# Unread matmuls ahead of the first and the eighth product of a two-layer graph-attention kernel

## The chip, the cores and the metric

The kernel runs on one NeuronCore of a Trainium2 chip. Five engines work side by side, each on its own queue of instructions in program order: TensorE (PE, matrix products; its weight loads are listed as PEld), VectorE (DVE), ScalarE (ACT), GpSimd (POOL), and SyncE (SP), which here issues the DMA transfers. Engines wait for each other through semaphores. The metric is the device time of one execution in microseconds (us); smaller is better. The kernel before takes 2812.2 us, the median of three runs (2810.62 to 2812.2).

## What is computed

128 graphs of 64 nodes with 768 features go through two layers. Layer 0 is a graph attention with 12 heads of 64 and a gate; layer 1 is a masked self-attention with 6 heads of 128. Each adds its input and normalizes.

```python
# layer 0
h = jnp.einsum('bnd,ade->bane', feat_in, W)
th = jnp.tanh(h)
attn = leaky(th @ w_src + swap(th @ w_dst)); softmax over masked neighbours
feat_out = elu(attn @ h + b)
gate = jax.nn.sigmoid(feat_in @ H_w.T + H_b)
x = _layernorm(x + gate * feat_out + (1.0 - gate) * feat_in)
# layer 1
q, k, v = x @ Wq + bq, x @ Wk + bk, x @ Wv + bv   # 6 heads
ctx = softmax(q @ k.T / sqrt(128) + bias) @ v
x = _layernorm(x + ctx @ Wf + bf)
```

(The formulas are shortened; all data are float32.)

## The kernel before

The rows are handled in pairs of tiles of 128 rows, 32 pairs in all; the code calls a pair p. In layer 0 the feature product and the gate product of a pair are one matrix product of 256 rows by 768 features by 1536 columns. It isn't computed block by block: a bilinear scheme writes it as **fifteen products**, `a0` to `a14` (the list `PRODUCTS`, lines 50 to 67), of sums of input blocks with sums of weight blocks. Each product is two matmuls of 128 x 512 columns (`Fifteen.product`, line 936) that accumulate into a bank of PSUM; what a product gives is then copied or accumulated into the tile `hg` by ACT (lines 962, 964) or DVE (line 960).

Three kinds of operands have to be there before a product may start:

- the input `xT` of the pair and the weight blocks `wa` come by DMA (lines 853 to 855). For the first pair, nothing can start before they land;
- the sums of input blocks, tiles `sx`, are made by DVE and POOL (`x_sums`, line 869);
- the sums of weight blocks are made once, by DVE, 17 of them (`MADE`, line 75, issued by `made(i)`, line 865, at line L867 of the profile), each over 128 x 1024 elements. One more, a negation, is made by ACT (line 863).

The products of the first pair run in the order of `EARLY[0]`, line 135: `a0 a5 a3 a8 a6 a1 a7 a10 a9 a2 a12 a4 a11 a14 a13`. The first is `a0`, the eighth is `a10`. The order of everything is written out by hand. The main loop (line 1364) goes through `items`, a list of products of all pairs; item i is issued to TensorE by `step`, which first issues the product and then the way out of the product before it. After item i, the acts that the dictionary `plan` holds for position i are issued to the other engines. For the first pair, the weight sums are planned there (line 1345): two at the outset, one to three after each of the items 0 to 5, and the last three (14, 15, 16) after items 7, 8 and 9. The eighth product, `a10`, reads the weight sum number 13 of the list (`MADE[13]`), which is planned after item 5. Position 7 of the loop is the eighth product of the first pair.

TensorE's part of a product therefore stands in its queue as early as the program has it; the semaphores it waits for are those of the operands above.

Three names matter for the change. `ident` (line 260) is the 128 x 128 identity, made by POOL at the start and used for transposes. `hb_bc` (line 856) is the gate's bias, 768 columns, repeated over the 128 partitions by a DMA. `bank("m", ...)` (line 248) hands out one of two PSUM banks that the transposes of the probabilities use later on.

Of the kernel before, what the change touches and what calls it, by code (L numbers as in the profile page):

```python
# [211 lines left out]
def kernel(  # L212
# [33 lines left out]
    V, S, G, T = nc.vector, nc.scalar, nc.gpsimd, nc.tensor  # L246

    def bank(tag, name, bufs=2):
        return ps.tile([P, 512], F32, tag=tag, name=name, bufs=bufs)
# [10 lines left out]
    ident = const.tile([P, P], F32, name="ident")  # L260
# [114 lines left out]
    def flush():  # L375
        for job, i in behind:
            job.way_out(i)
        behind.clear()

    def step(job, i):  # L380
        job.product(i)
        flush()
        behind.append((job, i))
# [432 lines left out]
    def drain(*sides):  # L816
        for s in sides:
            for _ in s:
                pass
# [4 lines left out]
    with ExitStack() as ph, ExitStack() as ph_r:  # L824
# [3 lines left out]
        def load_rows(pool, src, n, name):  # L828
            t = pool.tile([P, n], F32, name=name, bufs=1)
            nc.sync.dma_start(out=t, in_=src.partition_broadcast(P))  # L830
            return t
# [24 lines left out]
        hb_bc = load_rows(sbr, hb, D, "hb_bc")  # L856
# [5 lines left out]
        def negated():  # L862
            S.mul(wa[:, 0], wa[:, 14], -1.0)
# [5 lines left out]
        def x_sums(eng, p, ns):  # L869
            of = A.setdefault(p, {})  # L870
            x = xTs[p]

            def operand(o):
                if isinstance(o, tuple):
                    k, t = o
                    return x[:, 2 * k : 2 * k + 2, t * P : (t + 1) * P]
                return of[o]

            for n in ns:
                a, op, b = PRODUCTS[n][1]  # L880
                of[n] = sbr.tile([P, 2, P], F32, tag=f"sx{BUFFER[n]}", name=f"sx{n}_{p}", bufs=1)
                eng.tensor_tensor(of[n], operand(a), operand(b), op)  # L882
            for n in range(NW):
                if len(PRODUCTS[n][1]) == 2:
                    of[n] = operand(PRODUCTS[n][1])

        x_sums(V, 0, (6, 9, 2, 3, 0, 5))
        negated()
        x_sums(G, 0, (8,))
# [466 lines left out]
        def job_of(p, item):  # L1356
            if item[0] == "q":
                return jobs["q"]
            if (item[0], p) not in jobs:
                jobs[item[0], p] = Fifteen(p)  # L1360
            return jobs[item[0], p]

        rest = 0
        for i, (p, item) in enumerate(items):
            if i == new_at[NP - 1]:
                drain(summing)
            step(job_of(p, item), int(item[1:]))
            for _, acts in sorted(plan.get(i, ()), key=lambda entry: entry[0]):
                for act in acts:
                    act()  # L1370
            if new_at[3] <= i < new_at[NP - 1]:
                rest -= 1
                if rest <= 0:
                    rest = next(summing, 1)
            if item[0] == "q":
                jobs["rows"].ready(int(item[1:]) + 4)
# [153 lines left out]
```

## Time and profile before

| | |
|---|---|
| median of three runs | 2812.2 us |
| the profiled execution, its own time | 2813.49 us |
| its span in the profile | 2811.7 us |
| TensorE busy | 2776.4 us, 99% of the span |
| DVE, POOL, ACT busy | 66%, 52%, 48% |
| mean granted clock of TensorE | 0.997 |

A profile is one execution, recorded instruction by instruction; its times count from the start of the span. A line of a timeline gives the start, the duration of the group, the engine, the line of code, the operation, what it writes and reads with shapes, how many there are, and in brackets how long the engine had been idle before and what released it. Matmuls overlap in the array, so the durations of a group are longer than the distance from one start to the next; the distance is what TensorE can do at most. The granted clock is the share of TensorE's full clock that the chip gave it in a stretch.

At the start the transfers and the first sums of blocks come first; TensorE's first matmul starts at 7.86 us. After seven products it pauses, and goes on at 29.62 us with the eighth. The transfer of `hb_bc` is issued at 7.88 us. POOL finishes `ident` at 1.30 us.

### The profile page before, as it was taken

To read this page: it belongs to the slowest core of one execution; us is meant where nothing else is said; L and a number is where in the kernel's file an instruction comes from. 1 tells how busy PE (TensorE), PEld (TensorE's weight loads), DVE (VectorE), ACT (ScalarE), POOL (GpSimd) and SP (SyncE) were. 2 spreads that over 40 slices of the span, in tenths; PEclk is the share of its full clock that TensorE was granted. 3 is DMA by queue.
4 is the path that set the end of the run, shared out by engine and by line. 5 is a ranking of instruction groups with operands and counts; after the bars stand their busy time and mean duration, and the time that the engine had idled before them with its cause. 6 is when DMAs were issued, how large, how long until landed. Compare 5 with 4: busy or idle time off the path is not lost.

```text
span 2811.7 us, 47352 instructions
## 1 busy us (share of the span) xinstructions
PE 2776.4 (99%) x17472; PEld 1931.9 (69%) x17472; DVE 1851.2 (66%) x3215; ACT 1357.1 (48%) x3434; POOL 1453.7 (52%) x1501
## 2 busy tenths in 40 slices
PE   7999999999999999999999999999999999999998
PEld 3455555555555555555568888888888888888887
DVE  7867877777777777867764555555555555554557
ACT  4666676766767666676753222333222333221333
POOL 5556556565655656555454345445345435345435
PEclk9999999999999999999999999999999999999999
DMA  5354444544545445333444112222212222212212
GB/s 186 110 167 155 137 159 133 173 151 143 167 138 165 147 148 166 110 125 104 170 163 161 63 52 88 91 83 80 69 48 86 91 84 80 72 50 81 91 61 83
DMA packets 198038, 325.52 MB, mean 116 GB/s; under 512 B 46896, under 2 KB 125744, under 8 KB 197808
## 3 DMA queue, kind: packets, MB, share of 16 engines
q1 hardware_dynamic: 197520, 322.10, 34.8%
q8 instruction: 139, 2.28, 0.3%
q14 instruction: 91, 0.75, 0.1%
q10 hardware_dynamic: 288, 0.39, 0.0%
HBM read 198.48 MB, written 111.15 MB: 110 GB/s over the span
## 4 chain that ended last, share of the span: by engine, by line
PE 95%; DVE 1%; ACT 0%; issue 0%; DMA 0%; POOL 0%; ACTq 0%; DVEq 0%
PE y_a L944 18%; PE z_a L944 9%; PE z_q L524 9%; PE z_k L524 9%; PE y_v L345 9%; PE z_o L571 9%; PE y_k L524 6%; PE y_q L524 6%; PE y_o L571 6%; PE z_v L345 4%; PE x_v L345 2%; PE av L1099 2%; PE cp L689 2%; PE sp L629 2%; PE pTp L1078 2%; PE x1Tp L1078 1%
## 5 line engine op out<-in xcount | busy, mean ns | idle before, releaser
L944 PE MATMUL y_a<-wa,sx 128*128 128x512 f32 x1024 | 487.3, 605 | 19.2 <-DVE sx L882 7.9
L944 PEld LDWEIGHTS y_a<-wa,sx 128*128 128x128 f32 x1024 | 189.3, 192 | 221.6 <-issue 173.4
L488 POOL TENSOR_TENSOR so<-ctxT 128x256 f32<-128x256 f32 x224 | 157.7, 728 | 287.8 <-ACT ctxT L716 286.9
L716 ACT ACTIVATE ctxT<-cp,bv_c 128x256 f32<-128x256 f32 x192 | 73.8, 486 | 451.1 <-PE cp L689 451.1
L1129 POOL TENSOR_TENSOR x<-hg,x 128x768 f32<-128x768 f32 x64 | 111.8, 1748 | 211.1 <-ACT hg L1203 211.1
L524 PE MATMUL z_q<-xs,wa 128*128 128x256 f32 x896 | 211.9, 380 | 0.0
L655 ACT ACTIVATE sc<-sc 128x512 f32<-128x512 f32 x45 | 28.4, 630 | 379.7 <-DVE sc L652 379.7
L571 PE MATMUL z_o<-wf,so 128*128 128x256 f32 x896 | 209.3, 382 | 2.4 <-DVE y L584 2.4
L1037 ACT ACTIVATE att<-dd,sd 128x64 f32<-128x64 f32 x768 | 190.4, 336 | 33.4 <-DMA dd<-dstd 33.4
L986 POOL TENSOR_TENSOR th<-th,wsd 128x768 f32<-128x768 f32 x64 | 117.1, 1829 | 167.5 <-DVE th L985 167.5
L1066 ACT ACTIVATE prob<-att,mx 128x64 f32<-128x64 f32 x768 | 190.3, 335 | 25.8 <-DVE mx L1057 24.5
L524 PE MATMUL z_k<-xs,wa 128*128 128x256 f32 x840 | 198.5, 380 | 0.0
L397 POOL TENSOR_TENSOR rs_b<-ve_b,minus_half 128x1 f32<-128x1 f32 x64 | 40.9, 638 | 302.5 <-DVE ve_b L395 289.5
L584 DVE TENSOR_TENSOR y<-y,z_o 128x256 f32<-128x256 f32 x320 | 128.6, 419 | 100.3 <-PE z_o L571 100.2
L1051 DVE COPY_PREDICATED_SCALAR att<-nadj,neg 128x768 f32 x64 | 69.2, 1081 | 182.7 <-ACT att L1037 182.6
L571 PEld LDWEIGHTS z_o<-wf,so 128*128 128x128 f32 x896 | 169.1, 190 | 26.5 <-POOL so L488 2.6
L524 PEld LDWEIGHTS z_q<-xs,wa 128*128 128x128 f32 x896 | 170.2, 190 | 22.7
L944 PE MATMUL z_a<-wa,xT 128*128 128x512 f32 x384 | 183.1, 600 | 0.0
L524 PEld LDWEIGHTS z_k<-xs,wa 128*128 128x128 f32 x840 | 160.0, 190 | 21.3
L960 DVE TENSOR_TENSOR hg<-hg,y_a 128x512 f32<-128x512 f32 x225 | 151.9, 676 | 24.2 <-PE y_a L944 18.7
L760 POOL TENSOR_TENSOR y<-y,bf_bc 128x768 f32<-128x768 f32 x64 | 114.6, 1813 | 96.8 <-issue 56.0
L488 POOL TENSOR_TENSOR xs<-r,r 128x512 f32<-128x512 f32 x112 | 146.7, 1328 | 23.7 <-PE y_k L524 12.4
(154 smaller groups left out, 6427.1 us busy)
## 6 DMA issues: line engine op xcount, KB each, us to landing
xT<-in_xT_dram SPq DMA_DIRECT2D x32, 768.0 KB, 6.9
x<-in_x_dram SPq DMA_DIRECT2D x64, 384.0 KB, 3.4
dd<-dstd SPq DMA_DIRECT2D x128, 192.0 KB, 3.4
x1d<-x SPq DMA_DIRECT2D x64, 384.0 KB, 4.9
x1Td<-x1T SPq DMA_DIRECT2D x32, 768.0 KB, 4.8
vd<-v SPq DMA_DIRECT2D x64, 384.0 KB, 3.0
r<-x1Td SPq DMA_DIRECT2D x96, 256.0 KB, 3.2
v<-vd SPq DMA_DIRECT2D x192, 128.0 KB, 3.0
```

The source lines that it names most:

```text
L345: T.matmul(to[:, : self.n], lhsT, rhs, start=kc == 0 and not more, stop=kc == HK - 1, skip_group_check=more,)
L488: G.tensor_tensor(t, self.of(x[0]), self.of(x[2]), x[1])
L524: T.matmul(b[:, half * W2 : (half + 1) * W2], w[:, kc, half * P : (half + 1) * P], x[:, kc, :], start=half == kc == 0 and not more, stop=k ...
L571: T.matmul(b[:, :W2], x[:, kc, :], w[:, kc, :], start=kc == 0 and not more, stop=kc == 1, skip_group_check=more,)
L584: V.tensor_tensor(at, at, self.banks[path][:, :W2], ALU.add if sign > 0 else ALU.subtract)
L760: G.tensor_tensor(y, y, pools["bf"], ALU.add)
L944: T.matmul(b, x[:, kc, :], wa[:, n, kc, :], start=kc == 0 and not more, stop=kc == 1, skip_group_check=more,)
L960: V.tensor_tensor(at, at, b, ALU.add if sign > 0 else ALU.subtract)
L986: G.tensor_tensor(th[:, 1, :], th[:, 1, :], wsd[:, 1, :], ALU.mult)
L1037: S.activation(att3[:, a], dd3[:, a], AF.Prelu, bias=sd[:, H0 + a : H0 + a + 1], alpha=LEAKY)
L1066: S.activation(prob[:, at * N : (at + 1) * N], att[:, a * N : (a + 1) * N], AF.Exp, bias=mx[:, a : a + 1],)
L1129: G.tensor_tensor(xp, gate_of(t), xp, ALU.mult)
```

## The change

A helper `running` issues n matmuls of `ident` with an operand into a bank of the kind "m". Nothing reads what they write. It is called twice: before the sums of the first pair with n = 22 and `ident` itself as the operand (128 columns), and in the main loop ahead of item 7 with n = 20 and 512 columns of `hb_bc`.

```diff
+        def running(name, n, rhs):
+            b = bank("m", name)
+            for _ in range(n):
+                T.matmul(b[:, : rhs.shape[-1]], ident, rhs, start=True, stop=True)
+
+        running("warm", 22, ident)
         x_sums(V, 0, (6, 9, 2, 3, 0, 5))
         negated()
         x_sums(G, 0, (8,))
...
         for i, (p, item) in enumerate(items):
             if i == new_at[NP - 1]:
                 drain(summing)
+            if i == 7:
+                running("warm7", 20, hb_bc[:, :512])
             step(job_of(p, item), int(item[1:]))
```

The order of the instructions on DVE, ACT, POOL and SP is the same as before. On TensorE, the 22 stand ahead of everything and wait for POOL's `ident`; the 20 stand between `a7` and `a10` and wait for the transfer of `hb_bc`. What `a10` waits for is unchanged.

## The prediction

> **What bounds the kernel now.** I read the page's busy rows first, then the longest waits of TensorE, then its timeline over the first 45 us, then the granted clock in stretches of the same time.
>
> ```profile
> span 2811.7 us, 47352 instructions
> PE 2776.4 (99%) x17472; PEld 1931.9 (69%) x17472; DVE 1851.2 (66%) x3215; ACT 1357.1 (48%) x3434; POOL 1453.7 (52%) x1501
> ```
>
> TensorE (PE) is busy for 2776.4 of 2811.7 us, and the chain that ended last is 95% PE. So a microsecond put into PE's stream, or taken from it, reaches the end unless a later wait of PE swallows it. PE is idle for 35.3 us in all; the list of its waits says where:
>
> ```profile
> PE y_a L944 <- DVE sx L882: 7.9, 1, 7.9
> PE y_a L944 <- DVE wa L867: 7.8, 1, 7.8
> ```
>
> The columns are total, times, longest. These are the two places that the change fills, 15.7 us together. The timeline of PE (start, duration, then the group) shows what follows each of them:
>
> ```profile
> 7.86 3.67 PE L944 MATMUL y_a<-wa,sx 128*128 128x512 f32 x4 [7.86 <-DVE sx L882]
> 11.36 1.88 PE L944 MATMUL z_a<-wa,sx 128*128 128x512 f32 x4
> 13.08 5.31 PE L944 MATMUL y_a<-wa,sx 128*128 128x512 f32 x12
> 18.23 3.60 PE L944 MATMUL z_a<-wa,xT 128*128 128x512 f32 x8
> 29.62 6.44 PE L944 MATMUL y_a<-wa,sx 128*128 128x512 f32 x8 [7.79 <-DVE wa L867]
> 35.90 1.88 PE L944 MATMUL z_a<-wa,sx 128*128 128x512 f32 x4
> ```
>
> The reader is to see two things. First, a product of the fifteen leaves **four** records (a5 is the x4 at 11.36), though its code issues two matmuls: each 512-column float32 matmul is two records. Second, the pace: from 11.36 to 13.08 four records take 1.72 us, 0.429 us each; but from 7.86 to 11.36 four take 3.50 us (0.875 each), and from 29.62 to 35.90 eight take 6.28 us (0.785 each). After each wait PE runs slow for a while. The clock rows of the second place (stretch, length, busy PE, ..., granted clock, DMA share, GB/s) say why:
>
> ```profile
> 25.00:29.60 4.60, 0.00 (x0) 0.01 (x1) 4.57 (x5) 0.00 (x0) 0.40 (x1) 0.50 0.00 0
> 29.60:35.20 5.60, 5.58 (x7) 2.50 (x8) 4.37 (x7) 1.14 (x2) 1.85 (x2) 0.50 0.00 0
> 35.20:46.00 10.80, 10.80 (x26) 4.77 (x26) 7.99 (x8) 3.18 (x5) 7.16 (x6) 1.00 0.38 110
> ```
>
> The clock is halved from 25.0 to 35.2. At the first place the row says 1.00, but the spacing of the records is that of half clock; I go by the spacing.
>
> **The 20 matmuls at the eighth product.** Nothing is removed; 20 matmuls of 512 columns are issued between the seventh product (a7) and the eighth (a10). The room: a7's issue ends at 18.23 + 8 x 0.429 = 21.66, a10 starts at 29.62, so 7.96 us. The price: 20 matmuls x 2 records x 0.429 us = **17.16 us**. They keep the clock up, and the eight slow records of a10 and a9 go from 6.28 to 8 x 0.429 = 3.43 us, a gain of 2.85. But they are a 17.16 us queue in an 8 us hole, and a10 stands behind them on PE.
>
> Here a rule of the Trainium skill is weighed. Its page "TensorE: Matmul & The Clock Gate" (section "Wait — 56ns, not 53.3ns?") has 215.7 ns from one bf16 matmul of 512 columns to the next at full clock. With that, 20 would be 4.3 us, PE would again be idle before 29.62, and the change would be worth up to -2.85. But the records of this kernel are float32: 0.429 us, twice per matmul, 0.857 in all, which is the four passes that "FP8 and Floating Point Precision" (section "TensorE Precision Notes") gives for true FP32 (4 x 0.216 = 0.864). The trace has the duration, so I take 17.16. The first page's table "Why this matters for your kernels" asks for no gaps over some 3 us, and the halved clock after 25.0 agrees; the rule says nothing of a fill that outlasts its gap.
>
> Do the matmuls wait? Only for their operand hb_bc, whose transfer is issued at 7.88 and lands 10.0 later, at 17.9: no. Nobody reads their bank.
>
> **The 22 small ones at the start.** They wait for ident only, which POOL finishes at 1.30, so they start near 1.4. They are 44 records of 128 columns. The trace has no such float32 matmul; bounds: below, the six 128-column transposes (a single record each), at (0.82 - 0.27)/5 = 0.11 us; above, twice that, if a weight load could not lie beside a multiplication. The value matmuls of 64x65 decide it: 48 records over four quarters of the array start between 60.68 and 61.39, 0.06 us per record of a quarter, where 65/512 x 0.429 = 0.054 is the multiplication alone. So loads lie beside, and I take 0.11 at full clock, 0.22 at half.
>
> PE begins at half clock; at the first product full clock came after 3.5 us of work, at the eighth after 5.6. Full clock 3.4 to 6.8 us after 1.4 gives 15 to 31 slow records, then 29 to 13 at 0.11: the small ones end between **7.9 and 9.7**, about when or a little after the first operands are there (7.86). The first product then runs at full clock, 1.72 instead of 3.50 us, a gain of 1.78 less up to 1.8 of lateness.
>
> What is late next? The weight sums on DVE. a7 needs the seventh sum, which DVE (busy from 10.51 to 29.39 without waiting for PE) ends at 19.01. So a7 starts at 19.05 at the earliest (before: 19.95), and its issue ends at 20.8; if the small ones end at 9.7, at 9.7 + 28 x 0.429 = 21.7. Of this gain 0 to 0.9 us is left, and it counts, since the 20 start where a7 ends.
>
> **The sum.** The eighth product starts at 20.8 + 17.16 = 37.9 up to 38.9 instead of 29.62: +8.3 to +9.2. Less 2.85 for the clock: PE reaches the tenth product 5.5 to 6.4 us late, I take **+5.8** on the profiled execution.
>
> Does it last? DVE's accumulation at 33.41 waits for a10 and moves to about 40; the reduction and the two last weight sums behind it end near 46, while a11 and a13, which read them, start near 46.5 and 50. POOL's sums for the next pair wait for a10 and a9 and have 2.7 us to spare. From there ACT, DVE and POOL follow PE, so the whole schedule shifts.
>
> PE's later waits keep their cause:
>
> ```profile
> 59.07 0.69 DVE L960 TENSOR_TENSOR hg<-hg,y_a 128x512 f32<-128x512 f32 x1 [0.76 <-PE y_a L944]
> 71.88 1.99 PE L944 MATMUL y_a<-wa,xT 128*128 128x512 f32 x4 [0.84 <-DVE hg L960]
> 75.81 3.42 PE L944 MATMUL y_a<-wa,sx 128*128 128x512 f32 x4 [1.95 <-POOL sx L882]
> ```
>
> At 59.07 DVE itself is waiting for PE, so the DVE and POOL work that PE waits for at 71.88 and 75.81 moves with PE.
>
> **From the profile to the median.** The profiled execution took 2813.49 us (span 2811.7 and 1.8 around it), the median is 2812.2. The clock explains such a spread: PE also ran at half clock from 76.4 to 79.7 (granted 0.52), worth 1.65, and the slow stretch after the second wait may be worth 1.7 to 3.4 by when full clock comes. Without both, the profiled execution is 2813.49 - 2.85 - 1.65 = 2809.0. The changed kernel adds 8.3 to 9.2 to that, and in some executions 1.65: 2817.3 to 2819.9. The forecast is **2818.3 us**, 0.22% over the median; its own range is 2816.8 to 2820.2. A change of 0.2% (5.6 us, so 2817.8) is about what a measurement tells from none, and the forecast lies just beyond.
>
> **Rivals.**
> - *The small ones overrun too.* If their loads lie only half beside the multiplications (0.16 us a record), they end between 10 and 12, and everything moves 1.3 to 2.5 further: about 2820.5. For it: the trace has no 128-column float32 matmul. Against it: the 64x65 rows. Chance 0.10.
> - *Not slower: the delay is absorbed.* PE waits later for some 8 us between 45 and 185 us (DVE hg 2.3, POOL sx 1.9, x1T and sv and the rest 4). If DVE, POOL and ACT are by then behind on their own account and not on PE's, 6 us of delay let them catch up, the waits close, and the slow stretch at 76.4 goes: 2812.2 + 5.8 - 6 - 1 = 2811. For it: DVE is 91% busy and ACT 92% from 60 to 70. It decides from the point where the releaser's chain no longer ends in PE; at 59.07 it does, which is against it. Chance 0.08.
> - *The change does what it says.* If one of the 20 is one record of 0.429, they take 8.6 us, end near 29.4, and only the 2.85 is left: 2809.5. Against it: every product shows four records for two matmuls. Chance 0.03.
>
> **How the numbers follow.** The forecast has 0.79; some two thirds of it lie above 2817.8. Slower: 0.52 + 0.10 = 0.62. Within 0.2%: 0.26 and most of the absorbed case, 0.33. Faster: 0.05. The range from 2815.5 to 2821.0 takes in the forecast and most of the first rival, and leaves the last two out.
>
> **What would show it.** Right: 40 records ahead of the eighth product from about 21 to 38, full clock through, the a10 group at 0.429 spacing near 38, and the wait for POOL's sum near 81.5 still there. Wrong: the 20 ending before 30; the 44 small records ending after 10; the waits after 70 shrunk to nothing.

## The result, and the profile after

The changed kernel takes **2820.3 us** (median of 7 runs, 2818.64 to 2821.3); the kernel before, run beside it, 2811.68 us (7 runs, 2810.56 to 2812.92). The ratio is 1.0032, with a 95% interval of 1.0022 to 1.0042: slower by 8.6 us. The forecast was 2818.3 us, slower by 6.1.

The profiled execution took 2820.1 us, with a span of 2818.3. First the head of its page, then the timeline of TensorE (start, duration, group, idle time before it):

```profile
span 2818.3 us, 47520 instructions
PE 2795.1 (99%) x17556; PEld 1940.8 (69%) x17556; DVE 1845.7 (65%) x3215; ACT 1356.7 (48%) x3434; POOL 1456.6 (52%) x1501
```

```profile
1.36 7.66 PE L890 MATMUL warm<-ident 128*128 128x128 f32 x44 [1.36 <-POOL ident masks.py:199]
8.85 1.88 PE L950 MATMUL y_a<-wa,sx 128*128 128x512 f32 x4
10.57 1.88 PE L950 MATMUL z_a<-wa,sx 128*128 128x512 f32 x4
12.29 5.31 PE L950 MATMUL y_a<-wa,sx 128*128 128x512 f32 x12
17.44 3.81 PE L950 MATMUL z_a<-wa,xT 128*128 128x512 f32 x8
21.09 17.33 PE L890 MATMUL warm<-hb_bc,ident 128*128 128x512 f32 x40
38.26 3.60 PE L950 MATMUL y_a<-wa,sx 128*128 128x512 f32 x8
41.69 1.88 PE L950 MATMUL z_a<-wa,sx 128*128 128x512 f32 x4
```

The 22 are 44 records and end where the first product begins, at 8.85. The 20 are 40 records; from their start to the start of the eighth product are 38.26 - 21.09 = 17.17 us. The eighth and ninth product then take 41.69 - 38.26 = 3.43 us for eight records. The row of that stretch (start:end, length, busy PE, PEld, DVE, ACT, POOL, then the granted clock, the DMA share and GB/s) has full clock and no idle time of TensorE:

```profile
9.00:45.00 36.00, 36.00 (x85) 15.73 (x84) 26.36 (x25) 5.38 (x10) 11.46 (x9) 1.00 0.40 158
```

The two waits that the change was to fill, 7.9 and 7.8 us before, are gone from TensorE's list. Lines of the list after (total, times, longest):

```profile
PE y_a L950 <- DVE hg L966: 2.3, 2, 1.4
PE y_a L950 <- POOL sx L882: 1.9, 1, 1.9
...
PE warm L890 <- POOL ident masks.py:199: 1.4, 1, 1.4
PE z_v L345 <- DVE v L982: 1.0, 1, 1.0
PE y_v L345 <- ACT v L981: 1.0, 1, 1.0
```

The first two are as before. The third is the new wait of the 22 for the identity, 1.4 us at the very start. The last two are new as well: the wait of z_v for DVE was 0.2 before, and that of y_v for ACT was not in the list.

### The profile page after: what moved, and what is told of

Its sections match the earlier page's. It is cut to its first block, busy times and chain, and to the rows that moved or that the text cites. A ratio compares the mean times of both kernels' runs of the same rounds, so it can differ in the third digit from the quotient of the medians.

```text
span 2818.3 us, 47520 instructions
## 1 busy us (share of the span) xinstructions
PE 2795.1 (99%) x17556; PEld 1940.8 (69%) x17556; DVE 1845.7 (65%) x3215; ACT 1356.7 (48%) x3434; POOL 1456.6 (52%) x1501
## 4 chain that ended last, share of the span: by engine, by line
PE 92%; DVE 1%; DMA 1%; ACT 0%; issue 0%; SPq 0%; POOL 0%; ACTq 0%; DVEq 0%
PE y_a L950 17%; PE z_q L524 9%; PE z_k L524 9%; PE z_o L571 9%; PE z_a L950 9%; PE y_v L345 8%; PE y_k L524 6%; PE y_q L524 6%; PE y_o L571 6%; PE z_v L345 4%; PE x_v L345 2%; PE av L1105 2%; PE cp L689 2%; PE sp L629 2%; PE pTp L1084 1%; PE x1Tp L1084 1%
## 5 line engine op out<-in xcount | busy, mean ns | idle before, releaser
L950 PE MATMUL y_a<-wa,sx 128*128 128x512 f32 x1024 | 481.0, 598 | 3.6 <-POOL sx L882 1.9
```

Of the source, the lines that this page charges most:

```text
L950: T.matmul(b, x[:, kc, :], wa[:, n, kc, :], start=kc == 0 and not more, stop=kc == 1, skip_group_check=more,)
```

## The experiments

Theories were set against each other. **A**: the 20 are a queue that outlasts the wait, and apart from the clock nothing else matters. **B**: the 22 small ones delay the first product and are part of the loss. **C** and **D**: later waits grow or shrink, so that a delay at the start does not reach the end one to one. After the first four runs a fifth came up, **E**: TensorE's added instructions move the fetches of instructions (transfers that bring the program itself to the engine), and these delay small transfers of data.

### One part alone

The 22 without the 20:

```diff
-            if i == 7:
-                running("warm7", 20, hb_bc[:, :512])
```

> The 22 small matmuls alone. Theory A (the 20 are a queue that outlasts the wait, and nothing else of the change costs anything): no difference that can be measured, within 1 us of before; the first products run at full clock, a7 ends some 0.5 to 0.9 us earlier, but the eighth product still starts near 29.3 to 29.6, since DVE's weight sums set it; its wait grows to about 8.5 us and eight records still run at half clock. Rival B (the 22 delay the first product, and that delay is part of the loss): 1 to 2 us slower than before.

Measured: 2809.7 us against 2811.46 of before, ratio 0.9995 (0.9987 to 1.0003). No loss at all, so B, which expected 1 to 2 us, fell for the 22 alone. TensorE's wait for the eighth product's operand is still there:

```profile
28.90 5.60 PE L950 MATMUL y_a<-wa,sx 128*128 128x512 f32 x8 [7.79 <-DVE wa L867]
34.34 1.88 PE L950 MATMUL z_a<-wa,sx 128*128 128x512 f32 x4
```

The eight records take 34.34 - 28.90 = 5.44 us, where full clock would take 3.43, so they are still partly at half clock: here a filled first wait did nothing for the second.

The 20 without the 22:

```diff
-        running("warm", 22, ident)
```

> The 20 alone. Theory A: a7 ends at 21.7 as before, the 20 end at 38.8, the eighth product starts there at full clock; 9.2 later less 1.7 to 3.4 for the clock: about 6 to 7.5 us slower than before, and up to 1 us slower than the changed kernel with both. Rival B: 1 to 2 us faster than the changed kernel.

Measured: 2818.65 us, ratio 1.0026 (1.0016 to 1.0036). The eighth product starts at 39.23, 1.0 us later than with both, as A has it:

```profile
39.23 3.60 PE L949 MATMUL y_a<-wa,sx 128*128 128x512 f32 x8
```

But the end is 1.7 us **earlier** than with both (1.4 when each is taken against the kernel before that ran beside it). That is the size that B expected, and yet the 22 alone cost nothing. A misses something that happens after the eighth product.

### Fewer and more

```diff
-                running("warm7", 20, hb_bc[:, :512])
+                running("warm7", 9, hb_bc[:, :512])
```

> 22 small ones and 9 in place of 20. Theory A: 9 x 0.857 = 7.7 us end near 28.7, before the operand is there (29.3); the clock stays full; 1.7 to 3.4 us faster than before, about 2809. Theory C (a good part of the change's loss lies in later waits that grow, or in something other than the length of the queue): not faster than before, 2811 to 2813.

Measured: 2809.13 us, ratio 0.9991 (0.9983 to 0.9999). The eighth product starts at 28.97, 0.15 us after DVE has its operand, and eight records take 3.51 us. The median is 2.3 us below the kernel before, at the edge of what can be told. It can't be put down to this filling alone: the 22 alone came out 1.8 below, with the eight records still slow. In the timelines the filling is worth 5.44 - 3.51 = 1.93 us.

```profile
21.23 7.89 PE L890 MATMUL warm<-hb_bc,ident 128*128 128x512 f32 x18
28.97 3.67 PE L950 MATMUL y_a<-wa,sx 128*128 128x512 f32 x8
32.48 1.88 PE L950 MATMUL z_a<-wa,sx 128*128 128x512 f32 x4
```

With 30 in place of 20:

> 22 small ones and 30 in place of 20. Theory A: the ten more cost 10 x 0.857 = 8.6 us and all of it reaches the end: 8.6 us over the changed kernel, about 2829. Rival D (later waits absorb part of a delay): 3 to 7 us over the changed kernel.

Measured: 2828.85 us (ratio 1.0063, 1.0049 to 1.0077), 8.55 us over the changed kernel for ten matmuls. That is 0.855 us per matmul, against 0.857 in TensorE's stream: the length of the stream at the start is passed on to the end, and D (absorption, 3 to 7 us for the ten) fell. The agreement to 0.02 us is luck: there are four executions, 3 us apart, and later delays of 1 us and more come and go between kernels, as shown below.

The 9 without the 22:

> The 9 matmuls of 512 columns at the eighth product, without the 22. Theory A: the 22 bring nothing, since DVE's sums set the seventh and eighth product; a7 ends at 21.7, the 9 end at 29.4, at most 0.6 us after the operand is there; eight records at full clock: within 0.7 us of the kernel with 22 and 9 (2809.1). Rival (the 22 are what gains): near the kernel before, 2811.

Measured: 2810.12 us, ratio 0.9994 (0.9985 to 1.0002), 1.0 us over the kernel with both. Its eighth product starts at 30.24, later than the 29.4 expected, because full clock came only within the second product. So near the fitting size the 22 may help a little, by an earlier end of the seventh product; the difference is too small to be called shown.

### The same 20 in bf16

The 20 matmuls with bf16 tiles of ones as both operands instead of float32 (the memset that makes the tile is one instruction more on DVE):

```diff
+        ones16 = sbr.tile([P, 512], mybir.dt.bfloat16, name="ones16", bufs=1)
+        V.memset(ones16, 1.0)
+        def short(name, n):
+            b = bank("m", name)
+            for _ in range(n):
+                T.matmul(b, ones16[:, :P], ones16, start=True, stop=True)
...
-                running("warm7", 20, hb_bc[:, :512])
+                short("warm7", 20)
```

> 22 small ones, and the 20 of 512 columns on bf16 tiles of ones instead of the float32 bias. By the price that the Trainium skill gives for bf16 (215.7 ns), the 20 take 4.3 us and end near 25, some 4 us before the eighth product's operand. Theory A (what made the change slow is the float32 price of the 20): one record each, 0.215 us; the eighth product at 28.5 to 29.3; the clock stays up or drops for at most one slow stretch; within 1 us of the kernel with 22 and 9 (2809.1), and some 10 us faster than the changed kernel. Rival (any 20 there cost the time, by their count or by the instructions): slower than before.

Measured: 2809.89 us, ratio 0.9993 (0.9985 to 1.0001): 10.4 us faster than the changed kernel, with the same count of matmuls. Its timeline:

```profile
20.84 4.26 PE L898 MATMUL warm<-ones 128*128 128x512 bf16 x19
28.82 5.37 PE L958 MATMUL y_a<-wa,sx 128*128 128x512 f32 x8 [3.71 <-DVE wa L867]
```

One record per matmul (one of 20 is missing in the trace), 0.216 us apart; the 215.7 ns of the expectation are the figure of the Trainium skill's page "TensorE: Matmul & The Clock Gate", section "Wait — 56ns, not 53.3ns?", that the prediction cites, and the trace agrees. TensorE waits again for 3.71 us. The clock is halved from 29.42 on, 0.6 us after the end of that wait; the stretches show it:

```profile
25.00:29.40 4.40, 0.69 (x3) 0.38 (x3) 4.37 (x6) 0.00 (x0) 1.27 (x1) 1.00 0.00 0
29.40:32.80 3.40, 3.40 (x6) 1.34 (x5) 3.26 (x5) 1.14 (x2) 0.75 (x1) 0.50 0.00 0
```

So it is the element type that turned 20 matmuls from a fill that is too short into a queue that is too long, and the count of the added matmuls alone does not make the kernel slow.

### What is left: fetches and messages

Up to 45 us the profiles agree with A within about 1 us. To see where the rest comes from, the start of every matmul (counted from the last one backwards) was compared with the kernel before. For that the kernel before was profiled once more:

> The kernel before, profiled a second time. All theories: a time between 2809 and 2814. If the clock's slow stretches are what makes the executions differ, this one has a slow stretch after the second wait of 3.4 to 6.8 us, and the one after 75 us may be missing; its messages should be slow at the same places as in the first profile (theory E: the same instructions at almost the same times), at most a few differ.

Measured: 2809.5 us, below the median of the 26 beside it (2810.81); the slow stretch after the second wait lasted 6.8 us, the one near 76 us was missing. Its eighth product:

```profile
28.95 5.48 PE L944 MATMUL y_a<-wa,sx 128*128 128x512 f32 x8 [6.81 <-DVE wa L867]
```

Against this execution, TensorE is late by so many us at the places where it is itself at 44.6, 145.2, 180.2, 835, 1233 and 2799.7 us (a table worked out from the traces):

```
                        44.6  145.2  180.2   835   1233  2799.7
changed kernel           7.4    7.4    8.3   8.1    9.1    10.6
changed, again           7.7    8.6    9.6   9.3   11.1    11.9
20 alone                 8.4    9.0    9.0   8.6    8.5     8.5
40 of 256 columns        7.2    7.2    7.2   6.6    7.5     7.5
10 of 512, 20 of 256     6.7    7.5    8.4   8.0    9.7     9.7
20 in bf16              -0.2   -0.2    1.0   0.8    0.9     3.0
30 in place of 20       15.6   16.6   17.6  17.0   20.0    21.4
before, first profile    1.6    2.6    2.6   2.9    4.0     3.9
```

The changed kernel loses 7.4 us by the tenth product and a further 3.2, in steps of some 1 to 2 us with small gains between them, none of them after the first layer's end near 1440 us. The 20 alone are at 8.4 by then and end at 8.5: this is why they came out faster than both parts together. The bf16 kernel, whose queue is not too long, has late steps of 3.2 us as well (its profiled execution is its longest, 2812.5), so these are not a matter of the overrun.

The last row sets a limit to this. It is the same program as the base of the table, and it loses 1.0 us in the slow stretch near 76 us and 1.4 us more by 1233. Against that execution the changed kernel's further loss, from 145 us on, is 1.8 us instead of 3.2. Steps of 1 us after 180 us in single profiles therefore prove little by themselves.

The first step lies between 145 and 180. There z_v waits for DVE, DVE for ACT, and ACT for the message "dd": every tile sends a small tile of sums to DRAM (dstd<-sdT, 16 KB) and reads it back spread over all partitions (dd<-dstd). SyncE issues the second when the first has landed. The chain in the changed kernel:

```profile
152.28 2.98 ACT L1043 ACTIVATE att<-dd,sd 128x64 f32<-128x64 f32 x12 [1.50 <-DMA dd<-dstd]
156.11 0.96 DVE L1140 SCALAR_TENSOR_TENSOR ex<-ex,fo 128x768 f32<-128x768 f32 x1 [1.86 <-ACT ex L1129]
157.59 2.20 PE L345 MATMUL z_v<-wv,sv_v 128*128 128x384 f32 x6 [1.00 <-DVE v L982]
```

The DMA rows of the changed kernel from 140 to 152 us (queues with packets, MB, share; then one issue with count, size, us to landing):

```profile
q1 hardware_dynamic: 1369, 2.51, 62.3%
q8 instruction: 1, 0.02, 0.5%
q14 instruction: 1, 0.01, 0.2%
...
dstd<-sdT SPq DMA_DIRECT2D x1, 16.0 KB, 2.9
```

The message, issued at 145.09, took 2.9 us to land. Two fetches of instructions fall into that time: one on q8 (16 KB, at 145.96, for 0.97 us) and one on q14 (8 KB, at 147.21, for 0.31 us). The fetches on q8 are taken to be TensorE's: the kernel before has 139 of them, one for about 250 of its matmuls and weight loads. So E: in this kernel a fetch fell on a message. To test it, the added stream was made of other instructions of the same total length, which shifts all later fetches of TensorE:

```diff
-                running("warm7", 20, hb_bc[:, :512])
+                running("warm7", 40, hb_bc[:, :256])
```

> 22 small ones, and 40 matmuls of 256 columns in place of 20 of 512: the same time in TensorE's stream (80 x 0.214 = 17.2 us), but 80 instructions more[...]. Theory E (part of the loss over the sum lies in small messages through DRAM that are late when an instruction fetch falls on them): the eighth product starts within 0.4 us of the changed kernel's 38.3, but the slow messages are others, and the time moves by 0.7 to 2 us from the changed kernel's 2820.3, either way. Theory A (only the length of the queue and the clock): within 0.5 us of 2820.3.

Measured: 2817.88 us, ratio 1.0025 (1.0017 to 1.0034), 2.4 us less than the changed kernel, although its eighth product starts at 38.08, only 0.18 earlier. Taken against the kernel before that ran beside each, it is 7.1 against 8.6 us, 1.5 less, and the intervals of the two ratios overlap; but eight of its eleven executions are below all twelve of the changed kernel (the second measurement below included). Its DMA rows of the same window, and the first and last line of the chain:

```profile
q1 hardware_dynamic: 1499, 2.93, 74.7%
q14 instruction: 1, 0.01, 0.2%
...
dstd<-sdT SPq DMA_DIRECT2D x1, 16.0 KB, 1.7
```

```profile
151.13 2.97 ACT L1043 ACTIVATE att<-dd,sd 128x64 f32<-128x64 f32 x12 [0.54 <-DMA dd<-dstd]
156.55 2.20 PE L345 MATMUL z_v<-wv,sv_v 128*128 128x384 f32 x6
```

No fetch on q8 (that on q14 does not fall on the message), 1.7 us for the message, no wait of z_v, and no step at 145 in the table. A, which allowed 0.5 us, does not account for this; E is borne out at this place.

```diff
-                running("warm7", 20, hb_bc[:, :512])
+                running("warm7", 10, hb_bc[:, :512])
+                running("warm7h", 20, hb_bc[:, :256])
```

> 22 small ones, then 10 matmuls of 512 and 20 of 256 columns: again the same time in TensorE's stream as 20 of 512, with 40 instructions more. Theory E: as with 40 more, another set of slow messages, 0.7 to 2 us from 2820.3 either way, and not the same as with 80 more. Theory A: within 0.5 us of 2820.3.

Measured: 2819.92 us, ratio 1.0031 (1.0020 to 1.0041): 0.4 from the changed kernel, so by the total alone E missed. Its trace has the fetch on the message at 145 again (3.1 us to landing), and z_v waits 1.1 us again. Its later steps add up to 3.0 us, close to the changed kernel's 3.2; E as stated did not foresee that.

Is it chance? The changed kernel, profiled again:

> The changed kernel, profiled a second time. Theory E: the slow messages of its first profile (the one at 145 us among them, 2.9 us from issue to landing) are slow again, because the same instruction fetches fall on them; the wait of 1.0 us of the value product at 157 us is there again. Time within 1 us of 2820.3. Rival (they are chance): other messages are slow.

Measured: 2820.56 us, ratio 1.0033 (1.0021 to 1.0046); the message at 145 took 2.9 us, and z_v waited 1.2. There are 13 profiles of all kernels here, with 64 messages each. From its issue to the issue of the reading, which waits for it, a message takes 1.43 us in the median when no fetch is in flight (625 messages; 12% over 1.75), 2.23 when one on q8 is (109; 72% over 1.75), and 1.88 when only one on q14 is (98; 60%). Part of this is that the tiles differ: for one and the same tile, a fetch on q8 makes 0.34 us in the median, and the message is slower with it for 33 of 39 tiles. Nine of the 64 are over 1.75 in every profile. Of the others, the two profiles of the kernel before have the same seven, tiles 0, 25, 30, 38, 40, 48 and 58; the two of the changed kernel share 0, 5, 10, 25 and 28, and the second has three more. So most of the places belong to the program and not to the execution.

The message at 145 is that of tile 5. In five profiles it takes 2.7 us or more (changed, changed again, 10 and 20, 30, bf16), and these five have the wait of z_v (1.0 to 1.4 us) and the step; in the other eight it takes at most 2.1, z_v waits at most 0.4, and the table's step is missing or, in one profile (9 alone), 0.2. That a slow message makes the step is thus shown. That the fetch makes the message slow fits four of the five: in the bf16 kernel no fetch on q8 falls on it, and the one on q14 begins only 1.8 us after its issue. Nor does the number of slow messages decide: the changed kernel has five besides the nine, fewer than the kernel before, and the 20 alone have seven, only one of them among those of the kernel before, and yet no loss at the end.

### The wait near 75 us

```diff
-                running("warm7", 20, hb_bc[:, :512])
+                running("warm7", 9, hb_bc[:, :512])
...
+            if i == 29:
+                running("warm29", 2, hb_bc[:, :512])
```

> 22 small ones, 9 in place of 20, and 2 more (1.7 us) at the wait of 1.95 us ahead of the last product of the second pair, near 73 us. Theory: that wait sometimes brings the clock down for 3.4 us, which costs about 1 us; with the two it doesn't. 0 to 1 us faster than with 22 and 9 (2809.1), about 2808.7; slower by up to 1 us if the two delay the product.

Measured: 2809.25 us, ratio 0.9993 (0.9985 to 1.0001). The wait shrank to 0.23 us and the profile has no slow stretch there, but the median is that of 22 and 9. What it brings can't be told from nothing. The twelve other profiles, all with the full wait, have the slow stretch in five.

Of all versions only 22 and 9 has an interval that stays below 1, and only just.

## Why the prediction was right in direction and short in size

- **The price of the 20** (17.16 us) was right: 17.17. The figure of the page for bf16 (0.216 us measured) and the row of the trace (0.429, twice) were both right, each for its own element type; only the row was about this kernel.
- **The 22**, put at an end between 7.9 and 9.7: the first product started at 8.85, and in the other profiles with the 22 between 7.85 and 9.31. Its spacings were right too: the small records are 0.112 us apart at full clock and 0.213 at half, so the weight loads do lie beside the multiplications at 128 columns.
- **The start of the eighth product**, 37.9 to 38.9: 38.26. **The tenth product**, +5.8 on the profiled execution: 41.69 - 35.90 = 5.79.
- **From the profile to the median**: another execution of the kernel before gains less from the clock than the profiled one. In its second profile the eighth product started at 28.95, and the eight records took 34.26 - 28.95 = 5.31 us, so that 1.88 was to be gained instead of 2.85. The forecast had allowed for that (1.7 to 3.4), and took 2809.0 for the kernel without any slow stretch. From the second profile, 2809.5 with only 1.88 of slowness, the same working gives 2807.6; since the eighth product starts 0.67 earlier there, the 20 add 9.3 instead of 8.6, and the sum is 0.7 lower. Which execution is the typical one, two profiles don't show.
- **The step that failed** is "From there ACT, DVE and POOL follow PE, so the whole schedule shifts", with nothing added. The old waits did shift unchanged: the one for POOL's sum came at 81.62 instead of 75.81, with the same 1.95 us. But the shift grew afterwards: by 3.2 us between 145 and 1440 us in the changed kernel's profile, by 4.2 in its second, part of that a slow stretch at 82.6 (both against the second profile of the kernel before; against its first, 1.8 and 2.0 from 145 us on). The forecast put this term at nothing. With TensorE's 168 added instructions other messages were slow, and 0.9 us of the 3.2, the step near 145, is followed from the slow message to TensorE's wait; what made the rest stays open. Where the messages were slow much as in the kernel before (40 of 256 columns: of the places that are not slow everywhere, five of the seven of before are slow, and one other), the shift stayed at 7.5 and the time was 2817.88, next to the forecast's 2818.3.

Taken from the two profiles, the parts are 2807.6 + 9.3 + 3.2 = 2820.1, the time of the profiled execution. This is bookkeeping and no test, since the 3.2 is read from the same two profiles. That the forecast came within 2.0 us is in part luck: it had no term for the later steps, and with 40 matmuls of 256 columns in place of the 20, the same total length, these were only 0.3 us. The step near 1430 (TensorE waits 1.0 us for ACT) is in the profiles of the changed kernel, of 30 and of bf16, and missing in the changed kernel's second; a fetch falls on a message there too, but other large transfers are late as well, and it was not taken apart. Why a message is slower with a fetch in flight is not shown.

The rivals: absorption fell (30 in place of 20), the overrun of the small ones fell (they ended by 9.31 at the latest, not after 10), and the 20 as single records came true only in bf16.

## What to carry to other kernels

A filler in the queue of the bounding engine has to be counted in that engine's own time for its element type, and should end before the operand comes; what went beyond that was paid in full here (0.855 us for each further matmul). Count records in the trace, not matmuls in the code: here two records of 0.429 us per float32 matmul. When instructions are added to an engine, differences of 1 to 3 us can arise far away from the edit, here where small messages landed late; an edit of the same length with another count of instructions helps to tell such a difference from the price of the edit.

## What the runs showed that was not expected

- With an instruction fetch on q8 in flight, a 16 KB message through DRAM took 2.23 us instead of 1.43 in the median (0.34 us more for the same tile), and most of the slow places repeat from execution to execution. The Trainium skill ("Runtime: NRT & Kernel Launch", section "Instruction fetch mechanics") has fetches of 16 KB blocks whose cost is mostly hidden. The packets on q8 have that size, and no list of waits here shows TensorE waiting for instructions; for other transfers the cost seems not to be hidden.
- After a wait of only 1.95 us (with one of 0.84 some 4 us earlier) the clock was halved for 3.41 us in 5 of 12 profiles, from 0.35 to 1.3 us after TensorE had started to work again; after the wait of 3.71 us (bf16) it was halved 0.6 us after the restart. That these waits are the cause is argued from the order of events, not shown.
- With the 44 small records, full clock came between 2.9 and 6.2 us after their start (4.24 and 7.54 on the clocks of two profiles, start at 1.36).
